# Moving the gathers for q ahead of the previous sums in a sparse graph-attention kernel

## The chip, the cores and the metric

The kernel runs on one core of one Trainium2 chip. The metric is the device time of one execution in microseconds (us). Before the change it is 1331.45 us, the median of three runs (1329.03 to 1333.0). The profiled execution spans 1331.5 us.

A core has five engines with an instruction order each: TensorE (PE, matmuls, with its weight loads shown as PEld), VectorE (DVE), ScalarE (ACT), GpSimd (POOL, which here issues the gathers) and SyncE (SP). Transfers run on 16 DMA engines.

## The reference

One attention layer over a sparse graph with 3327 nodes and 1024 features, with a normalised input and a residual. Cut to what matters:

```python
# x: (3327, 1024) f32; adj: (3327, 3327) int32, 0/1, symmetric, with the diagonal, about 17 ones a row
h = jnp.maximum(_layernorm(x, axis=-1), 0.0)
f = h @ Wf + bf
g = h @ Wg + bg
e = jax.nn.relu(f @ g.T)
scores = jnp.where(adj > 0, e, NEG)            # NEG = -9e15
attention = jax.nn.softmax(scores, axis=1)
x = x + attention @ (h @ W + bW)
```

Only the scores at the edges matter. So the kernel makes q = h A + v with A = Wf Wg^T (and the bias terms) once per node, takes the dot product of q with the rows h of the neighbours only, and sums these rows with the softmax's weights before it multiplies by W.

## The kernel before

The first part (0 to about 260 us) makes, for every node, the normalised row (`hd` in DRAM), the list of its neighbours (`pd`), and the matrix A. It sorts the nodes by degree into 26 tiles of 128 nodes; `perm[:, s]` holds the nodes of tile s. CAPS holds the largest number of neighbours of each tile, and ORDER the order in which the tiles are worked on:

```python
CAPS = [37, 25, 23, 22, 21, 21, 20, 20, 19, 19, 18, 18, 17, 17, 17, 16, 16, 15, 15, 15, 14, 14, 13, 13, 12, 11]
ORDER = [24, *range(24), 25]
ONE_CHUNK = 16
AHEAD = 3
```

The second part, which the change touches, works on one tile after the other. A tile with more than 16 neighbours is worked on in two halves; a half, or a whole small tile, is a "unit". The loop:

```python
    prepare(ORDER[0])
    prepare(ORDER[1])
    dots_of_first(ORDER[0], CAPS[ORDER[0]])
    ...
    for i, (s, k0, k1) in enumerate(units):
        last = k1 == CAPS[s]
        at = ORDER.index(s)
        dots(s, range(k0, k1))                  # gathers of neighbours' rows, dot products with q (DVE)
        softmax(s, k0, k1, last)                # exponential on ACT, the rest on DVE
        if i + 1 < len(units):
            s2, a, b = units[i + 1]
            dots(s2, range(a, min(b, a + AHEAD)))   # the first three of the next unit
        if last and at:
            finish(ORDER[at - 1])               # scatter the results of the tile before
        combine(s, k0, k1, last)                # weighted sum of the rows
        if last:
            project(s)                          # times W; adds x
            if at + 2 < NT:
                prepare(ORDER[at + 2])          # q of the tile two ahead
            ...
```

`prepare` gathers the neighbours' list `pi` and the tile's own rows `hp`, transposes these on PE and multiplies them by A:

```python
    psp = ctx.enter_context(tc.tile_pool(name="ps", bufs=2))       # pi
    gpool = ctx.enter_context(tc.tile_pool(name="G", bufs=26))     # all gathered rows, hp too
    qpool = ctx.enter_context(tc.tile_pool(name="q", bufs=2))
    hTpool = ctx.enter_context(tc.tile_pool(name="hT", bufs=1))

    def gather(to, table, idx, **kw):
        return nc.gpsimd.indirect_dma_start(out=to, ..., in_=table, ...)   # profile line L686

    def transposed2(to, of):
        for g in range(0, KD, 4):
            ps = p_t.tile([P, 4, P], FP, name="ps_t")
            for k in range(4):
                nc.tensor.transpose(ps[:, k, :], of[:, (g + k) * P : (g + k + 1) * P], ident)   # L698
            nc.scalar.copy(to[:, g : g + 4, :], ps)                                             # L699

    def prepare(s):
        e = st[s] = {}
        pi = psp.tile([P, PW], I32, name="pi")
        gather(pi, pd[:, :], perm[:, s : s + 1])
        hp = gpool.tile([P, D], FP, name="G")
        gather(hp, hd[:, :], perm[:, s : s + 1])
        hT = hTpool.tile([P, KD, P], FP, name="hT")
        transposed2(hT, hp)
        q = e["q"] = qpool.tile([P, QW], FP, name="q")
        for i, o in enumerate(range(0, QW, QB)):
            ...                                  # 8 matmuls hT x A_sb into ps_q (L731), copied to q by ACT (L735)
        ...                                      # the mask, from pi (L740)
        e["edges"] = [pi[:, k : k + 1] for k in range(KL)]
        ...                                      # longer lists, for tiles 0 and 1 only
```

The work on a neighbour k, the softmax, and the sums:

```python
    def dot(s, k):
        g = G[s, k] = gpool.tile([P, D], FP, name="G")
        st["gathered"] = gather(g, hd[:, :], e["edges"][k])
        nc.vector.tensor_tensor_reduce(junk, g, e["q"][:, :D], ...)                # L767

    def softmax(s, k0, k1, last):
        ...                                                                        # max on DVE: nm, L796
        nc.scalar.activation(sc, sc, AF.Exp, bias=nm, accum_out=l)                 # L800
        ...
        nc.vector.reciprocal(rs, l)                                                # L807
        ...

    def combine(s, k0, k1, last):
        ...
            if k in pe:                          # some neighbours: scaled on ACT, summed on PE
                nc.scalar.activation(g, g, AF.Copy, scale=p)                       # L842
                sum_transposed(e, g, e["first"], False)                            # 8 matmuls yT_ps, L826
            elif k == 0:
                nc.scalar.activation(y, y, AF.Copy, scale=p)                       # L846
            else:                                # the others: summed on DVE
                nc.vector.scalar_tensor_tensor(y, g, p, y, ...)                    # L848

    def project(s):
        sum_transposed(e, e["y"], e["first"], True)                                # yT_ps, L826
        ...                                                                        # yT, copied by ACT, L855
        for o in range(OH):
            ...                                  # 8 matmuls yT x W_sb into ps_o (L861), copied to res by ACT (L870)
        ...
            gather(r, x[:, :], perm[:, s : s + 1], compute_op=ALU.add)             # res += x
```

`finish(s)` scatters `res` to `out` (L881) and is told to be issued after the last neighbour's gather that stands before it in the source.

Of the kernel before, what the change touches and what calls it, by code (L numbers as in the profile page):

```python
# [8 lines left out]
FP = mybir.dt.float32  # L9
I32 = mybir.dt.int32  # L10
# [18 lines left out]
ORDER = [24, *range(24), 25]  # L29
# [264 lines left out]
def edge_path(ctx: ExitStack, tc: tile.TileContext, x, adj, Wf, bf, Wg, bg, W, bW, out, flag):  # L294
# [12 lines left out]
    N, D = x.shape  # L307
    O = W.shape[1]
    P = 128
# [4 lines left out]
    NT = (N + P - 1) // P  # L314
    OH = O // CB
    SW = -(-N // SEG)
    PW = KL + 1
# [13 lines left out]
    hd = dram.tile([N, D], FP, name="hd")  # L331
    pd = dram.tile([N, PW], I32, name="pd")
# [11 lines left out]
    perm = const.tile([P, NT], I32, name="perm")  # L344
# [6 lines left out]
    with ExitStack() as part1:  # L351
# [288 lines left out]
        ps = p_mm.tile([P, CB], FP, name="ps_A")  # L640
# [27 lines left out]
    nc.sync.dma_start(W_sb, W.rearrange("(k p) o -> p k o", p=P))  # L668
    bWb = ctx.enter_context(tc.tile_pool(name="bW", bufs=1)).tile([P, O], FP, name="bWb")
    nc.sync.dma_start(bWb, bW[None, :].to_broadcast([P, O]))  # L670
    psp = ctx.enter_context(tc.tile_pool(name="ps", bufs=2))
    gpool = ctx.enter_context(tc.tile_pool(name="G", bufs=26))
    mpool = ctx.enter_context(tc.tile_pool(name="more", bufs=1))
    qpool = ctx.enter_context(tc.tile_pool(name="q", bufs=2))
# [10 lines left out]
    def gather(to, table, idx, **kw):  # L685
        return nc.gpsimd.indirect_dma_start(  # L686
            out=to,
            out_offset=None,
            in_=table,
            in_offset=bass.IndirectOffsetOnAxis(ap=idx, axis=0),  # L690
            **kw,
# [9 lines that stand above are left out]
    st = {}  # L701
# [4 lines left out]
    def filled(pool, name, row, w, at):  # L706
        ps = pool.tile([P, CB], FP, name=name)
        if at < 2:
            nc.tensor.matmul(ps, ident, A_sb[:, 0, :CB], start=True, stop=True)
        o = at * w % row.shape[1]  # L710
        nc.scalar.copy(ps[:, :w], row[:, o : o + w])
        banks[name, at] = ps

    for at in range(2):
        filled(p_q, "ps_q", vb, QB, at)
        filled(p_o, "ps_o", bWb, CB, at)

    def prepare(s):
        e = st[s] = {}
        pi = psp.tile([P, PW], I32, name="pi")  # L720
        gather(pi, pd[:, :], perm[:, s : s + 1])
        hp = gpool.tile([P, D], FP, name="G")
        gather(hp, hd[:, :], perm[:, s : s + 1])
        hT = hTpool.tile([P, KD, P], FP, name="hT")
        transposed2(hT, hp)
        q = e["q"] = qpool.tile([P, QW], FP, name="q")
        for i, o in enumerate(range(0, QW, QB)):
            at = 3 * ORDER.index(s) + i
            ps = banks.pop(("ps_q", at))
            for k in range(KD):  # L730
                nc.tensor.matmul(  # L731
                    ps[:, :QB], hT[:, k, :], A_sb[:, k, o : o + QB], start=False, stop=(k == KD - 1),
                    skip_group_check=True,
                )
            nc.scalar.copy(q[:, o : o + QB], ps[:, :QB])  # L735
            if at + 2 < 3 * NT:
                filled(p_q, "ps_q", vb, QB, at + 2)
        df = pi.bitcast(FP)[:, KL : KL + 1]
        mask = e["mask"] = small.tile([P, KM], FP, name="mask")
        nc.vector.tensor_scalar(mask, iotak, df, NEG, op0=ALU.is_ge, op1=ALU.mult)  # L740
        e["sc"] = small.tile([P, KM], FP, name="sc")
        if s == NT - 1:
            e["x"] = gpool.tile([P, O], FP, name="G")
            gather(e["x"], x[:, :], perm[:, s : s + 1])
        e["edges"] = [pi[:, k : k + 1] for k in range(KL)]
        if s >= MORE:
            return

        ct = xpool.tile([P, O], FP, name="res")[:, : SEG * 8]
        gather(ct, cd[:, :], perm[:, s : s + 1])  # L750
        found = mpool.tile([P, KM - KL + 8], FP, name="found")
        for i in range(0, KM - KL + 8, 8):
            nc.vector.max(found[:, i : i + 8], ct)
            if i < KM - KL:
                nc.vector.match_replace(ct, found[:, i : i + 8], ct, 0.0)
        more = mpool.tile([P, KM - KL], I32, name="more")
        nc.vector.tensor_scalar(more, found[:, 8:], 1.0, -1.0, op0=ALU.max, op1=ALU.add)
        e["edges"] += [more[:, k : k + 1] for k in range(KM - KL)]

    G = {}  # L760

    def dot(s, k):
        e = st[s]
        g = G[s, k] = gpool.tile([P, D], FP, name="G")
        st["gathered"] = gather(g, hd[:, :], e["edges"][k])
        junk = jpool.tile([P, D], BF, name="junk")
        nc.vector.tensor_tensor_reduce(  # L767
            junk, g, e["q"][:, :D], 1.0, e["q"][:, D : D + 1], op0=ALU.mult, op1=ALU.add,
            accum_out=e["sc"][:, k : k + 1],
        )  # L770

    def dots_of_first(s, cap):

        e = st[s]
        for k in range(cap):
            G[s, k] = gpool.tile([P, D], FP, name="G")
            st["gathered"] = gather(G[s, k], hd[:, :], e["edges"][k])
        sums = mpool.tile([P, 3, cap], FP, name="sums")
        for i, o in enumerate(range(0, D, QB)):
            w = min(QB, D - o)  # L780
            for k in range(cap):
                junk = jpool.tile([P, D], BF, name="junk")
                nc.vector.tensor_tensor_reduce(
                    junk[:, :w], G[s, k][:, o : o + w], e["q"][:, o : o + w], 1.0,
                    e["q"][:, D : D + 1] if o + w == D else 0.0, op0=ALU.mult, op1=ALU.add,
                    accum_out=sums[:, i, k : k + 1],
                )
        nc.vector.tensor_reduce(e["sc"][:, :cap], sums.rearrange("p c k -> p k c"), AX.X, ALU.add)

    def softmax(s, k0, k1, last):  # L790

        e = st[s]
        sc = e["sc"][:, k0:k1]
        nc.vector.scalar_tensor_tensor(sc, sc, 0.0, e["mask"][:, k0:k1], op0=ALU.max, op1=ALU.add)
        nm = small.tile([P, 1], FP, name="nm")
        nc.vector.tensor_reduce(nm, sc, AX.X, ALU.max, negate=True)  # L796
        if k0:
            nc.vector.tensor_tensor(nm, nm, e["nm"], op=ALU.min)
        l = small.tile([P, 1], FP, name="l")
        nc.scalar.activation(sc, sc, AF.Exp, bias=nm, accum_out=l)  # L800
        if k0:
            al = small.tile([P, 1], FP, name="al")
            nc.scalar.activation(al, e["nm"], AF.Exp, bias=nm, scale=-1.0)
            nc.vector.scalar_tensor_tensor(l, e["l"], al, l, op0=ALU.mult, op1=ALU.add)
        if last:
            rs = small.tile([P, 1], FP, name="rs")
            nc.vector.reciprocal(rs, l)  # L807
            if k0:
                nc.vector.tensor_tensor(al, al, rs, op=ALU.mult)
            nc.vector.tensor_scalar(sc, sc, rs, None, op0=ALU.mult)  # L810
        if k0:
            nc.scalar.activation(e["y"], e["y"], AF.Copy, scale=al)
        e["nm"], e["l"] = nm, l
# [64 lines left out]
    def finish(s):  # L878

        with tc.issue_after(st["gathered"].ins):  # L880
            ins = nc.gpsimd.indirect_dma_start(  # L881
                out=out[:, :],
                out_offset=bass.IndirectOffsetOnAxis(ap=perm[:, s : s + 1] if s < N // P else final, axis=0),
                in_=st[s]["r"],
                in_offset=None,
                bounds_check=None if s < N // P else N - 1,
                oob_is_err=s < N // P,
            )
        tc.declare_no_dep(ins.ins, group="results", reason="other rows")
        tc.add_to_no_dep_group("results", ins.ins)  # L890
# [19 lines left out]
    def dots(s, ks):  # L910
        for k in ks:
            if (s, k) not in done:
                done.add((s, k))
                dot(s, k)

    prepare(ORDER[0])
    prepare(ORDER[1])
    dots_of_first(ORDER[0], CAPS[ORDER[0]])
    done.update((ORDER[0], k) for k in range(CAPS[ORDER[0]]))
    for i, (s, k0, k1) in enumerate(units):  # L920
        last = k1 == CAPS[s]
        at = ORDER.index(s)
        dots(s, range(k0, k1))
        softmax(s, k0, k1, last)
        if i + 1 < len(units):
            s2, a, b = units[i + 1]
            dots(s2, range(a, min(b, a + AHEAD)))
        if last and at:
            finish(ORDER[at - 1])
        combine(s, k0, k1, last)  # L930
        if last:
            project(s)
            if at + 2 < NT:
                prepare(ORDER[at + 2])
            if at + 2 == NT - 1:
                bad = failed()
# [41 lines left out]
```

## Time and profile before

| engine | busy us | share of the span | instructions |
|---|---|---|---|
| PE | 1105.4 | 83% | 4312 |
| PEld | 690.2 | 52% | 4312 |
| DVE | 1184.0 | 89% | 2377 |
| ACT | 580.1 | 44% | 923 |
| POOL | 847.2 | 64% | 677 |

"Busy" is the time in which an engine has an instruction at work. The profile names an instruction by its line in the kernel (L698), its engine, its operation, and the tiles it writes and reads: `ps_t<-ident,G` is a transpose of a gathered row tile. `G<-hd,pi` is a gather of neighbours' rows by a list `pi`, `G<-hd,perm` the gather of a tile's own rows for q, `pi<-pd,perm` the gather of the lists. What stands in square brackets behind an instruction in the timeline is how long its engine stood idle ahead of it, and what it waited for. A row of the waits gives the instruction, what it waited for, the sum in us, the number of waits and the longest one.

### The profile page before, as it was taken

The numbers are of one execution on the slowest core, as the hardware profiler recorded it, in microseconds if no ns is written. First come the engines' busy times: TensorE is split into PE (matmuls) and PEld (weight loads), VectorE is DVE, ScalarE is ACT, GpSimd is POOL, SyncE is SP. The second block draws the span as 40 slices with busy tenths as digits, with TensorE's granted clock in tenths as the row PEclk, the third lists the DMA queues.
The fourth block names the chain that finished last, engine by engine and source line by source line (L and its number), as shares of the span: only waits on it lengthen the run. The fifth ranks groups of instructions, "written<-read, shape, count | busy, mean of one in ns | idle before, by whom it ended". The sixth has DMA issues, their size and how long they took to land. (4 is left out here: it accounts for less than half of the span.)

```text
span 1331.5 us, 14117 instructions
## 1 busy us (share of the span) xinstructions
PE 1105.4 (83%) x4312; PEld 690.2 (52%) x4312; DVE 1184.0 (89%) x2377; ACT 580.1 (44%) x923; POOL 847.2 (64%) x677
## 2 busy tenths in 40 slices
PE   2588897289249899898999999999999997889965
PEld 2355564056136655566555656656556554545532
DVE  4779888749988999999999999999999998889990
ACT  6778787224125533555334444444433332224210
POOL 6699888356657766666666766666665655666511
PEclk9589898589669999999999999999999998899978
DMA  9999996398659988998899888988788776868811
GB/s 356 338 374 342 393 374 218 134 376 309 207 177 333 337 284 297 330 316 308 297 313 321 319 291 309 311 296 297 263 290 284 259 253 222 269 198 274 303 32 50
DMA packets 101660, 374.45 MB, mean 281 GB/s; under 512 B 14731, under 2 KB 18474, under 8 KB 98247
## 3 DMA queue, kind: packets, MB, share of 16 engines
q0 software_dynamic: 79584, 286.77, 63.4%
q1 hardware_dynamic: 11004, 71.01, 14.0%
q10 hardware_dynamic: 10986, 15.67, 3.3%
q8 instruction: 36, 0.59, 0.2%
q14 instruction: 50, 0.41, 0.1%
HBM read 344.11 MB, written 29.30 MB: 280 GB/s over the span
## 5 line engine op out<-in xcount | busy, mean ns | idle before, releaser
L686 POOL DMA_INDIRECT G<-hd,pi x454 | 487.4, 1074 | 199.2 <-issue 102.6
L767 DVE CUSTOM_DVE_ANT_0 junk<-G,q 128x1024 bf16<-128x1024 f32 x456 | 586.5, 1286 | 8.8 <-DMA G<-hd,pi 4.3
L731 PE MATMUL ps_q<-A_sb,hT 128*128 128x342 f32 x1248 | 382.1, 460 | 11.8 <-ACT hT L699 11.7
L848 DVE SCALAR_TENSOR_TENSOR G<-G,sc 128x1024 f32<-128x1024 f32 x296 | 381.4, 1289 | 10.6 <-ACT G L846 6.8
L861 PE MATMUL ps_o<-W_sb,yT 128*128 128x512 f32 x832 | 364.4, 596 | 7.9 <-ACT yT L855 7.9
L731 PEld LDWEIGHTS ps_q<-A_sb,hT 128*128 128x128 f32 x1248 | 236.2, 193 | 136.5 <-ACT hT L699 17.8
L861 PEld LDWEIGHTS ps_o<-W_sb,yT 128*128 128x128 f32 x832 | 158.0, 191 | 202.0 <-issue 187.5
L424 POOL TENSOR_TENSOR r<-r,iotaj 128x1664 f32<-128x1664 f32 (+3 forms) x52 | 191.6, 3724 | 31.9 <-ACT r L417 31.8
L826 PE MATMUL yT_ps<-ident,G 128*128 128x128 f32 x1376 | 172.5, 281 | 28.6 <-DVE G L848 15.3
L826 PEld LDWEIGHTS yT_ps<-ident,G 128*128 128x128 f32 x1376 | 155.8, 144 | 55.3 <-ACT G L842 26.4
L842 ACT ACTIVATE G<-G,sc 128x1024 f32<-128x1024 f32 x146 | 154.9, 1136 | 0.0
L475 DVE MAX8 cand<-r 128x8 f32<-128x208 f32 (+2 forms) x416 | 121.7, 360 | 29.0 <-POOL r L424 29.0
L551 PE MATMUL ps_A<-WgT,WfT 128*128 128x342 f32 x432 | 140.5, 485 | 0.2 <-ACT WfT L532 0.2
L870 ACT COPY res<-ps_o 128x512 f32<-128x512 f32 x50 | 29.2, 585 | 255.0 <-PE ps_o L861 252.8
L551 PEld LDWEIGHTS ps_A<-WgT,WfT 128*128 128x128 f32 x432 | 86.3, 205 | 60.5 <-issue 21.1
L735 ACT COPY q<-ps_q 128x342 f32<-128x342 f32 x78 | 34.3, 440 | 172.7 <-PE ps_q L731 158.7
L698 PE MATMUL ps_t<-ident,G 128*128 128x128 f32 x208 | 31.9, 303 | 80.1 <-DMA G<-hd,perm 67.5
L881 POOL DMA_INDIRECT out_dram<-res,perm x25 | 35.6, 1424 | 84.0 <-DMA res<-in_x_dram,perm 83.7
L417 ACT ACTIVATE r<-r 128x3327 f32<-128x3327 int32 (+4 forms) x28 | 77.8, 2781 | 1.5 <-ACT xt L461 0.5
L686 POOL DMA_INDIRECT res<-in_x_dram,perm x25 | 43.1, 1724 | 54.8 <-ACT res L870 49.9
L698 PEld LDWEIGHTS ps_t<-ident,G 128*128 128x128 f32 x208 | 27.3, 157 | 88.8 <-issue 74.5
L699 ACT COPY hT<-ps_t 128x512 f32<-128x512 f32 x52 | 29.2, 588 | 100.4 <-PE ps_t L698 100.4
(132 smaller groups left out, 669.4 us busy)
## 6 DMA issues: line engine op xcount, KB each, us to landing
r<-in_adj_dram SPq DMA_DIRECT2D x25, 1663.5 KB, 10.9
xt<-in_x_dram SPq DMA_DIRECT2D x25, 512.0 KB, 9.2
hd<-xt ACTq DMA_DIRECT2D x25, 512.0 KB, 7.7
G<-hd,pi POOLq DMA_INDIRECT x454, 6.2
wr<-in_L_gnn_Wg_dram SPq DMA_DIRECT2D x8, 512.0 KB, 5.8
wr<-in_L_gnn_Wf_dram SPq DMA_DIRECT2D x8, 512.0 KB, 8.1
W_sb<-in_L_gnn_W_dram SPq DMA_DIRECT2D x1, 4096.0 KB, 17.9
cd<-cand ACTq DMA_DIRECT2D x25, 64.0 KB, 7.6
```

What stands on the lines that cost most here:

```text
L417: nc.scalar.activation(r[:n, b:e], a[:n, b:e], AF.Sign, accum_out=to)
L424: nc.gpsimd.tensor_mul(r[:n, b:e], r[:n, b:e], iotaj[:n, : e - b])
L475: nc.vector.max(cand[:n, s * 8 : s * 8 + 8], r[:n, s * SW : min(N, (s + 1) * SW)])
L551: nc.tensor.matmul(ps[:, :QB], WfTs[c][:, k, :], WgT[:, k, o : o + QB], start=(k == 0), stop=(k == KD - 1))
L686: return nc.gpsimd.indirect_dma_start(out=to, out_offset=None, in_=table, in_offset=bass.IndirectOffsetOnAxis(ap=idx, axis=0), **kw,)
L698: nc.tensor.transpose(ps[:, k, :], of[:, (g + k) * P : (g + k + 1) * P], ident)
L731: nc.tensor.matmul(ps[:, :QB], hT[:, k, :], A_sb[:, k, o : o + QB], start=False, stop=(k == KD - 1), skip_group_check=True,)
L767: nc.vector.tensor_tensor_reduce(junk, g, e["q"][:, :D], 1.0, e["q"][:, D : D + 1], op0=ALU.mult, op1=ALU.add, accum_out=e["sc"][:, k : k ...
L826: nc.tensor.matmul(e["yT"][:, c, :], g[:, c * P : (c + 1) * P], ident, is_transpose=True, start=(first and c % 4 == 0), stop=(last and c % ...
L842: nc.scalar.activation(g, g, AF.Copy, scale=p)
L848: nc.vector.scalar_tensor_tensor(y, g, p, y, op0=ALU.mult, op1=ALU.add)
L861: nc.tensor.matmul(ps, yT[:, k, :], W_sb[:, k, o * CB : (o + 1) * CB], start=False, stop=(k == KD - 1), skip_group_check=True,)
```

## The change

The two gathers at the head of `prepare` become a function of their own, `fetch`. It is called behind the softmax of the last unit of a tile, for the tile two ahead: in front of the first three gathers of the next unit, the scatter of results, the sums and the product with W. `prepare` stays where it was and finds list and rows fetched. As the list of the tile two ahead may now be fetched while the list of the present tile and that of the next are held, the lists get three buffers in place of two. The purpose is to have the rows at hand when TensorE comes to transpose them.

```diff
--- before.py
+++ after.py
@@ -668,7 +668,7 @@
     nc.sync.dma_start(W_sb, W.rearrange("(k p) o -> p k o", p=P))
     bWb = ctx.enter_context(tc.tile_pool(name="bW", bufs=1)).tile([P, O], FP, name="bWb")
     nc.sync.dma_start(bWb, bW[None, :].to_broadcast([P, O]))
-    psp = ctx.enter_context(tc.tile_pool(name="ps", bufs=2))
+    psp = ctx.enter_context(tc.tile_pool(name="ps", bufs=3))
     gpool = ctx.enter_context(tc.tile_pool(name="G", bufs=26))
     mpool = ctx.enter_context(tc.tile_pool(name="more", bufs=1))
     qpool = ctx.enter_context(tc.tile_pool(name="q", bufs=2))
@@ -715,14 +715,19 @@
         filled(p_q, "ps_q", vb, QB, at)
         filled(p_o, "ps_o", bWb, CB, at)
 
+    def fetch(s):
+
+        e = st[s] = {}
+        pi = e["pi"] = psp.tile([P, PW], I32, name="pi")
+        gather(pi, pd[:, :], perm[:, s : s + 1])
+        hp = e["hp"] = gpool.tile([P, D], FP, name="G")
+        gather(hp, hd[:, :], perm[:, s : s + 1])
+
     def prepare(s):
-        e = st[s] = {}
-        pi = psp.tile([P, PW], I32, name="pi")
-        gather(pi, pd[:, :], perm[:, s : s + 1])
-        hp = gpool.tile([P, D], FP, name="G")
-        gather(hp, hd[:, :], perm[:, s : s + 1])
+        e = st[s]
+        pi = e["pi"]
         hT = hTpool.tile([P, KD, P], FP, name="hT")
-        transposed2(hT, hp)
+        transposed2(hT, e["hp"])
         q = e["q"] = qpool.tile([P, QW], FP, name="q")
         for i, o in enumerate(range(0, QW, QB)):
             at = 3 * ORDER.index(s) + i
@@ -913,7 +918,9 @@
                 done.add((s, k))
                 dot(s, k)
 
+    fetch(ORDER[0])
     prepare(ORDER[0])
+    fetch(ORDER[1])
     prepare(ORDER[1])
     dots_of_first(ORDER[0], CAPS[ORDER[0]])
     done.update((ORDER[0], k) for k in range(CAPS[ORDER[0]]))
@@ -922,6 +929,8 @@
         at = ORDER.index(s)
         dots(s, range(k0, k1))
         softmax(s, k0, k1, last)
+        if last and at + 2 < NT:
+            fetch(ORDER[at + 2])
         if i + 1 < len(units):
             s2, a, b = units[i + 1]
             dots(s2, range(a, min(b, a + AHEAD)))
```

## The prediction

> **What bounds the kernel now.** I read the page first, then a table of stretches, then the waits and the timelines of the stretch where an engine stands still. The page gives VectorE (DVE) 89% of the span and TensorE (PE) 83%, and neither average says where a change can act. The table of stretches does. Its columns are the stretch, its length, and the busy time of PE, weight loads, DVE, ScalarE (ACT), GpSimd (POOL), each with a count, then the granted clock, the DMA share and GB/s.
>
> ```profile
> 480.00:900.00 420.00, 397.37 (x1660) 250.64 (x1659) 418.33 (x654) 191.33 (x304) 281.85 (x260) 0.99 0.90 309
> 900.00:1100.00 200.00, 192.88 (x753) 119.09 (x752) 190.52 (x274) 76.07 (x129) 122.07 (x108) 1.00 0.82 273
> 1100.00:1200.00 100.00, 80.66 (x281) 49.34 (x280) 81.05 (x120) 26.36 (x49) 57.92 (x50) 0.90 0.72 232
> ```
>
> From 480 to 900 us DVE is idle for 420.00 - 418.33 = 1.7 us. Nothing that only moves a gather can win there. From 900 to 1100 PE is at 96% and DVE at 95%: both are nearly full. From 1100 to 1200 both drop to 81%, although POOL and the DMA engines have room. That is the place to look. The waits of DVE in the stretch from 1085 to 1230 us name what stops it:
>
> ```profile
> DVE rs L807 <- ACT sc L800: 17.8, 3, 6.2
> DVE G L848 <- ACT G L846: 0.7, 1, 0.7
> ```
>
> Three waits, 17.8 us, all at the reciprocal after the softmax's exponential. ACT is not busy there (26.36 of 100 us), so something holds it up in its own order. The timelines of PE and of POOL show the first case:
>
> ```profile
> 1111.78 1.51 PE L698 MATMUL ps_t<-ident,G 128*128 128x128 f32 x6 [8.59 <-DMA G<-hd,perm]
> 1113.08 1.91 PE L826 MATMUL yT_ps<-ident,G 128*128 128x128 f32 x8
> ...
> 1116.27 13.90 PE L861 MATMUL ps_o<-W_sb,yT 128*128 128x512 f32 x32
> ```
>
> ```profile
> 1123.33 0.59 ACT L870 COPY res<-ps_o 128x512 f32<-128x512 f32 x1 [6.74 <-PE ps_o L861]
> 1123.95 0.59 ACT L711 COPY ps_o<-bWb 128x512 f32<-128x512 f32 x1
> 1124.48 0.30 ACT L800 ACTIVATE sc<-sc,nm 128x15 f32<-128x15 f32 x1
> ```
>
> The row `ps_t` is the transpose of the rows that make q. It waited 8.59 us for its gather. Behind it in PE's order stand the last sum of tile 18 (`yT_ps`) and tile 18's product with W (`ps_o`). Behind that product in ACT's order stands the exponential of tile 19, and DVE waits for that one 6.25 us. So one late gather of q's rows blocks three engines in turn. The same happens at 1152.16 us (PE waits 6.14, DVE 5.55) and at 1190.48 (4.55 and 6.04). DVE: 6.25 + 5.55 + 6.04 = 17.84 us. PE: 8.59 + 6.14 + 4.55 = 19.28 us.
>
> Why is the gather late? POOL's timeline before the second case:
>
> ```profile
> 1134.93 0.97 POOL L686 DMA_INDIRECT G<-hd,pi  x1 [0.30 <-issue]
> 1139.21 1.42 POOL L881 DMA_INDIRECT out_dram<-res,perm  x1 [3.31 <-DMA res<-in_x_dram,perm]
> 1141.26 1.75 POOL L686 DMA_INDIRECT G<-hd,pi  x1 [0.63 <-issue]
> 1143.32 0.94 POOL L686 DMA_INDIRECT G<-hd,pi  x1 [0.30 <-issue]
> 1144.56 0.94 POOL L686 DMA_INDIRECT G<-hd,pi  x1 [0.30 <-issue]
> 1145.80 0.95 POOL L686 DMA_INDIRECT pi<-pd,perm  x1 [0.31 <-issue]
> 1147.06 0.94 POOL L686 DMA_INDIRECT G<-hd,perm  x1 [0.30 <-issue]
> ```
>
> I take 1134.93 for the last gather of tile 20. Then come the scatter of results, which waits for its rows, the first three gathers of tile 21, the list `pi` of tile 22, and only then the rows for q of tile 22. PE, whose order has these transposes next, starts them at 1152.16, 5.1 us after the gather was issued.
>
> **What the Trainium skill says.** "Perfetto Trace Analysis", section on the SWDGE DMA instruction: the profiled end of such an instruction is the end of descriptor generation, and not of the data movement. The trace agrees: 0.94 us for the instruction, a median of 6.2 us to landing for `G<-hd,pi`. "DMA: Bandwidth & Descriptors", rules for kernel authors: to overlap a DMA with compute, issue it early and wait late. That is what the change tries, and the 8.59 us of PE is what the present place costs. "Perfetto Trace Analysis", optimization strategy: a gap that repeats on the engine that should be saturated can mean that there is no room for the next tile's buffer. In part this holds: `pi` waited 24.0 us in 11 cases for the landing of gathers that read the buffer it takes, which the third buffer cures. The rows for q need no list, though, and their delay in the lines above is one of place.
>
> **The change, part by part.** No instruction is added or removed: 26 list gathers, 26 row gathers and all matmuls stay. What moves is the place of two gathers per tile (24 of the 26 tiles; the first two keep theirs) and a wait for a buffer.
>
> 1. *How much sooner.* For tile 22 the three gathers of tile 21 no longer stand in front: issued at 1141.26, 1143.32 and 1144.56, with `pi` at 1145.80, they take 4.5 us. If the scatter also stays behind, `pi` can go right after 1134.93 + 0.97 = 1135.90, and the rows at 1135.90 + 0.30 + 0.95 + 0.30 = 1137.5, which is 9.6 us sooner. So 4.5 to 9.6 us. For tile 21, where four gathers stand between 1099.16 and the list at 1105.21, three of them out of the way make 1105.21 - 1100.43 = 4.8 us. For tile 23 the list went out at 1175.83 and the rows at 1182.71, behind two gathers and the gather of x; right behind the list is 1177.2, or 5.5 us sooner.
> 2. *What that is worth.* For tile 21 the wait of 8.59 us would still be 3.8; the sums of tile 18 were ready at 1105.2 (end of the last DVE sum), so they start some 4.6 us sooner than 1113.08, and DVE's 6.25 us shrink by 4.6. For tile 22 PE's 6.14 us shrink by 4.5 to 6.14, DVE's 5.55 by 4.5 to 5.55: I take 5.2. For tile 23 PE's 4.55 us go, DVE gets 4.5 of its 6.04. Sum: 4.6 + 5.2 + 4.5 = 14.3 us. DVE is full around these waits (28.93 of 29 us between two of them), so I count them on the path at full value.
> 3. *The start.* The rows for tile 2 went out at 378.93, behind gathers issued at 368.86, 373.19 and 375.59, and PE stood 42.59 us for them. But DVE was busy 38.24 of the 40 us from 340 to 380, so these 42.59 us are not on the path. Only a later wait of DVE for ACT, 2.73 us at 394.74, hangs on the transposes: I count 1 us of it.
> 4. *What it costs.* The next tile's first three gathers go out two instructions later, 2 x 1.25 = 2.5 us. In the tail they have room: issued at 1141.26, first used by DVE at 1153.42, 12.2 us for a landing of 6.2. At the start they have little: DVE waited there 4.3 us in four waits for gathers (401 to 415 us), and 1 us may be added. The rows hold one of the 26 buffers of G some 5 to 10 us longer per tile of 35 us, 0.2 of a buffer on average: I count 0.5 us.
> 5. *Order.* The order on the engines is fixed when the program is built and isn't that of the source: transposes for tile 21 stand before tile 18's product. With the gather earlier, the whole order is made anew, and some waits will come back at another place. I take off 1.5 us for that.
>
> Sum: 14.3 + 1 - 1 - 0.5 - 1.5 = 12.3 us, some 13 with the shortened waits for lists. From 1331.45 us that makes 1318 us.
>
> **Rivals.** *(a) PE becomes the bound.* From 900 to 1100 us PE is at 96%, and a tile there costs it 14.07 (ps_q) + 13.90 (ps_o) + 1.04 (ps_t) + some 4 (sums) = 33 us, as much as DVE's 15 x 1.33 + 11 x 1.2 = 33. If PE ran on without a gap, DVE would wait for it instead. Against it: PE loses the same 19.28 us of idle, and after 1200 its tiles follow at 28 to 29 us. If this came true in full, half of the gain would go: 1325. *(b) The gather isn't in front where it matters.* Rows need a buffer of G, and POOL waits for those (67.9 us for DVE's sums to release them; 11.21 us at 1129.24). If the buffer and not the place is the limit, the rows come no sooner: 1330. Against it: in the lines above the three gathers in front got their buffers at once (waits of 0.30 and 0.63). *(c) The new order is worse.* A transpose that is believed ready too soon can be put even further ahead of sums and products, and stall PE for the buffer of hT or for the rows again. Each such stall cost 5 to 6 us of DVE; three or four more in a tail of ten tiles make 1345 to 1350. *(d) More than the three waits.* If the early hold-ups (2.73 + 4.3 us at the start) go as well, and all of 17.84, it is 1307.
>
> **Range and chances.** I give (a) 0.25, (b) 0.15, (c) 0.12 with mild and bad forms, the main line and (d) the rest. Main line with its neighbours spans 1312 to 1325; (d) sets the lower end at 1306, a mild (c) the upper at 1331. Two per cent are 26.6 us, more than all of 17.84 + 2.73 + 4.3 = 24.9 us of waits that I can point at, so faster by over 2% needs a gain that I don't see: 0.10. Slower by over 2% (1358) needs the bad form of (c): 0.04. Within: 0.86.
>
> **What would show each step right or wrong.** Step 1: rows for q of tiles 20 to 23 issued ahead of the next tile's first gathers, and the wait of `ps_t` for `G<-hd,perm` after 900 us down from 19.3 to under 6. Step 2: DVE's wait of `rs` for `sc`, 17.8 us in three cases, down to under 5, and DVE at 93% or more from 1100 to 1200. Step 3: the 42.6 us of PE at the start shorter by about 10, with DVE's busy share there as it was. Step 4: DVE's wait for gathers near 4 to 6 us in all. The lists' wait for landings, 24.0 us, near 0. The prediction is wrong if `rs` still waits 10 us or more, if PE's wait moves to another operand with DVE waiting as long, or if DVE's idle time between 480 and 900 grows beyond 5 us.

## The result, and the profile after

The changed kernel takes 1312.75 us (median of five runs, 1309.46 to 1315.63), 18.7 us less than before: 0.986 of the time before, with a 95% interval of 0.984 to 0.988. The prediction was 1318 us, a gain of 13.4. The profiled execution spans 1309.4 us; it lies 22.1 us under that of the kernel before, more than the medians do, as the one execution was slower than its kernel's median and the other faster. Behind `fetch` the line numbers are five higher: L826 is now L831, L861 is L866, and L807 is L812.

The table of stretches (stretch, length, busy time of PE, weight loads, DVE, ACT and POOL with counts, granted clock, DMA share, GB/s):

```profile
480.00:900.00 420.00, 397.33 (x1658) 250.75 (x1657) 418.20 (x655) 192.69 (x306) 298.68 (x262) 0.99 0.91 313
900.00:1100.00 200.00, 190.06 (x747) 117.81 (x745) 190.55 (x274) 75.75 (x129) 120.34 (x108) 1.00 0.80 267
1100.00:1200.00 100.00, 96.61 (x348) 58.26 (x349) 98.53 (x143) 32.51 (x57) 63.77 (x56) 0.98 0.82 280
```

The first two stretches are as before. In the third DVE goes from 81.05 to 98.53 us and PE from 80.66 to 96.61. DVE's waits from 1063 to 1208 us, the counterpart of the stretch shown before:

```profile
DVE rs L812 <- ACT sc L805: 1.2, 2, 0.9
DVE G L853 <- ACT G L851: 1.2, 1, 1.2
```

The 17.8 us of three waits are down to 1.2, the longest to 0.9. The timeline of PE at the transposes of tiles 21, 22 and 23 (the bracket gives the stand ahead and its cause):

```profile
1102.07 0.95 PE L698 MATMUL ps_t<-ident,G 128*128 128x128 f32 x6 [3.78 <-DMA G<-hd,perm]
1102.82 1.91 PE L831 MATMUL yT_ps<-ident,G 128*128 128x128 f32 x8
...
1106.09 13.90 PE L866 MATMUL ps_o<-W_sb,yT 128*128 128x512 f32 x32
...
1135.69 1.04 PE L698 MATMUL ps_t<-ident,G 128*128 128x128 f32 x8
...
1167.64 1.04 PE L698 MATMUL ps_t<-ident,G 128*128 128x128 f32 x8
```

The first stand of 8.59 us is 3.78 now, the second (6.14 us) and the third are gone. And POOL's timeline around the rows of tile 22:

```profile
1124.76 0.97 POOL L686 DMA_INDIRECT G<-hd,pi  x1 [0.30 <-issue]
1128.37 0.97 POOL L886 DMA_INDIRECT out_dram<-res,perm  x1 [2.65 <-DMA res<-in_x_dram,perm]
1129.65 0.96 POOL L686 DMA_INDIRECT G<-hd,perm  x1 [0.30 <-issue]
1130.92 2.00 POOL L686 DMA_INDIRECT G<-hd,pi  x1 [0.30 <-issue]
1133.22 0.94 POOL L686 DMA_INDIRECT G<-hd,pi  x1 [0.30 <-issue]
1134.47 0.94 POOL L686 DMA_INDIRECT G<-hd,pi  x1 [0.30 <-issue]
```

The rows now stand right behind the scatter, 1.28 us after its start, and the three gathers of tile 21 follow. Before, they came 1147.06 - 1139.21 = 7.85 us after it. The list, which has a third buffer, went out well ahead, at 1112.04.

Where the time went can be read off without any model, because the order of DVE's instructions is the same in both kernels, instruction for instruction. So each softmax can be set against itself. The table gives the start of the DVE instruction that opens it (L794, now L799), in us after the first one (308.38 before, 306.60 now; the 1.8 us ahead of that lie in the first part, which the change doesn't touch):

| softmax of | before | changed | difference |
|---|---|---|---|
| tile 24 | 0 | 0 | 0 |
| tile 1, first half | 102.89 | 100.57 | -2.3 |
| tile 19 | 807.43 | 804.37 | -3.1 |
| tile 20 | 844.83 | 836.51 | -8.3 |
| tile 21 | 882.04 | 867.43 | -14.6 |
| tile 22 | 916.76 | 896.17 | -20.6 |
| tile 25, the last | 971.21 | 950.60 | -20.6 |

Of 20.6 us, 17.5 are won in three steps of 5.3 to 6.3 us behind the softmax of tiles 19, 20 and 21, 2.3 at the start, and 0.8 little by little between.

### The profile page after: what moved, and what is told of

Its sections match the earlier page's. It is cut to its first block, busy times and chain, and to the rows that moved or that the text cites. A ratio compares the mean times of both kernels' runs of the same rounds, so it can differ in the third digit from the quotient of the medians.

```text
span 1309.4 us, 14125 instructions
## 1 busy us (share of the span) xinstructions
PE 1105.0 (84%) x4312; PEld 691.6 (53%) x4312; DVE 1182.3 (90%) x2377; ACT 580.3 (44%) x923; POOL 857.4 (65%) x677
## 4 chain that ended last, share of the span: by engine, by line
DVE 33%; issue 25%; DMA 14%; PE 13%; POOL 8%; ACT 6%; POOLq 0%; ACTq 0%; DVEq 0%; SPq 0%
DVE G L853 16%; DMA G<-hd,pi 7%; DVE junk L772 6%; POOL G L686 5%; DVE cand L475 4%; PE yT_ps L831 4%; PE ps_o L866 3%; PE ps_q L736 3%; PE ps_A L551 2%; POOL r L424 2%; ACT G L847 2%; DVE sc L772 1%; DMA res<-in_x_dram,perm 1%; ACT r L417 1%; DMA r<-in_adj_dram 1%
## 5 line engine op out<-in xcount | busy, mean ns | idle before, releaser
L686 POOL DMA_INDIRECT G<-hd,pi x454 | 498.2, 1097 | 201.5 <-issue 99.8
L736 PE MATMUL ps_q<-A_sb,hT 128*128 128x342 f32 x1248 | 374.7, 454 | 13.8 <-ACT hT L699 13.8
L866 PE MATMUL ps_o<-W_sb,yT 128*128 128x512 f32 x832 | 367.3, 600 | 9.2 <-ACT yT L860 9.2
L736 PEld LDWEIGHTS ps_q<-A_sb,hT 128*128 128x128 f32 x1248 | 233.0, 190 | 136.0 <-ACT hT L699 19.7
L866 PEld LDWEIGHTS ps_o<-W_sb,yT 128*128 128x128 f32 x832 | 158.8, 192 | 205.1 <-issue 189.0
L831 PE MATMUL yT_ps<-ident,G 128*128 128x128 f32 x1376 | 176.7, 286 | 37.4 <-ACT G L847 20.7
L831 PEld LDWEIGHTS yT_ps<-ident,G 128*128 128x128 f32 x1376 | 161.2, 148 | 62.9 <-ACT G L847 35.3
```

What stands on the lines that cost most here:

```text
L686: return nc.gpsimd.indirect_dma_start(out=to, out_offset=None, in_=table, in_offset=bass.IndirectOffsetOnAxis(ap=idx, axis=0), **kw,)
L736: nc.tensor.matmul(ps[:, :QB], hT[:, k, :], A_sb[:, k, o : o + QB], start=False, stop=(k == KD - 1), skip_group_check=True,)
L831: nc.tensor.matmul(e["yT"][:, c, :], g[:, c * P : (c + 1) * P], ident, is_transpose=True, start=(first and c % 4 == 0), stop=(last and c % ...
L866: nc.tensor.matmul(ps, yT[:, k, :], W_sb[:, k, o * CB : (o + 1) * CB], start=False, stop=(k == KD - 1), skip_group_check=True,)
```

## The experiments

Two theories stood against each other at first. **Place of the rows**: the rows for q come in time because they are gathered ahead of the next tile's first three gathers; the rest of the change is not needed. **Room for the lists**: the third list buffer takes away the 24.0 us that POOL waited for lists, and that is the gain. The edit of e1 is to the kernel before, all others are to the changed kernel. Ratios are to the kernel before on the same chip, with 95% intervals; they leave out executions in a slower state of the chip, so they can differ from the ratio of the medians. On the chips of e5 to e8, e11 and e12 even the kernel before took 1373 to 1376 us, and the traces of these runs have long stands of ScalarE for which they name no cause. Their times are a result about these chips, taken up at the end; they cannot tell the theories apart.

### e1: three list buffers alone

```diff
-    psp = ctx.enter_context(tc.tile_pool(name="ps", bufs=2))
+    psp = ctx.enter_context(tc.tile_pool(name="ps", bufs=3))
```

> The kernel before with three list buffers in place of two and nothing moved. Theory 'place of the rows' (the gain comes from the rows for q being gathered ahead of the next tile's first three neighbour gathers): the rows keep their place behind those three, so 1331 us within 4, and DVE still waits 15 to 18 us for the exponential after 1100 us. Theory 'room for the lists' (the lists' 24 us of waits for a free buffer hold GpSimd up): most of the gain is here, 1313 to 1318 us. Some small gain from lists alone: 1326 to 1330.

Measured: 1332.79 us, ratio 1.001 (1.000 to 1.002). The waits for lists of the whole execution, first in the kernel before, then here:

```profile
POOL pi L686 <- DMA G<-hd,pi: 24.0, 11, 2.9
```

```profile
POOL pi L686 <- DMA G<-hd,pi: 6.3, 3, 3.6
```

And those of DVE from 900 us on:

```profile
DVE rs L807 <- ACT sc L800: 17.6, 6, 7.0
```

POOL's wait for lists falls from 24.0 to 6.3 us, and the time doesn't move. DVE waits as before.

### e2: only the rows early

```diff
     def fetch(s):
         e = st[s] = {}
-        pi = e["pi"] = psp.tile([P, PW], I32, name="pi")
-        gather(pi, pd[:, :], perm[:, s : s + 1])
         hp = e["hp"] = gpool.tile([P, D], FP, name="G")
         gather(hp, hd[:, :], perm[:, s : s + 1])
     def prepare(s):
         e = st[s]
-        pi = e["pi"]
+        pi = psp.tile([P, PW], I32, name="pi")
+        gather(pi, pd[:, :], perm[:, s : s + 1])
```

The lists have two buffers here.

> Only the gather of the rows moves to the new place; the list's gather stays in prepare, with two list buffers. 'Place of the rows': all of the gain, 1312 to 1316 us, DVE's wait for the exponential under 3 us. 'Room for the lists': no gain, 1328 to 1333 us.

Measured: 1314.34 us, ratio 0.986 (0.984 to 0.988), the ratio of the whole change. DVE's wait for the exponential from 900 us on is 2.5 us.

### e3: only the list early

```diff
     def fetch(s):
         e = st[s] = {}
         pi = e["pi"] = psp.tile([P, PW], I32, name="pi")
         gather(pi, pd[:, :], perm[:, s : s + 1])
-        hp = e["hp"] = gpool.tile([P, D], FP, name="G")
-        gather(hp, hd[:, :], perm[:, s : s + 1])
     def prepare(s):
         e = st[s]
         pi = e["pi"]
+        hp = e["hp"] = gpool.tile([P, D], FP, name="G")
+        gather(hp, hd[:, :], perm[:, s : s + 1])
```

> Only the gather of the list moves, with three list buffers; the gather of the rows stays in prepare. 'Place of the rows': 1328 to 1333 us, DVE's three waits for the exponential as before, 15 to 18 us. 'Room for the lists': 1313 to 1318 us.

Measured: 1332.95 us, ratio 1.001 (1.000 to 1.002), with 14.8 us of waits for the exponential from 900 us on, in the trace of the fastest execution: nothing is won.

### e4: both early, two list buffers

```diff
-    psp = ctx.enter_context(tc.tile_pool(name="ps", bufs=3))
+    psp = ctx.enter_context(tc.tile_pool(name="ps", bufs=2))
```

> The changed kernel with two list buffers in place of three: both gathers in the new place. 'Place of the rows': the third buffer is not needed, 1311 to 1315 us, equal to the changed kernel's 1312.75 within its spread; GpSimd may wait again some 10 to 25 us for lists, off the path. 'Room for the lists': 1325 to 1332 us.

Measured: 1314.77 us, ratio 0.986 (0.983 to 0.989). The wait for lists, over the whole execution:

```profile
POOL pi L686 <- DMA G<-hd,pi: 44.0, 13, 4.4
```

POOL waits longer for lists than in any other of these kernels, 44.0 us, more than I had expected, and the kernel is as fast as the changed one within the intervals. With e1 and e3 this settles that "room for the lists" is wrong: taking that wait away wins nothing, and nearly doubling it costs nothing that shows.

### e5 and e9: the new place for the last five tiles alone

```diff
-        if last and at + 2 < NT:
+        if last and at + 2 < NT and at + 2 >= 21:
             fetch(ORDER[at + 2])
 ...
             if at + 2 < NT:
+                if not (at + 2 >= 21):
+                    fetch(ORDER[at + 2])
                 prepare(ORDER[at + 2])
```

> The changed kernel, but list and rows go to the new place only for the last five tiles worked on (21, 22, 23 and 25, and 20); for all tiles before, both gathers stay at the head of prepare. If the gain is the three removed waits of the tail: 1314 to 1318 us, with TensorE still standing over 40 us for the rows near 342 us. If the gain is spread over all tiles or comes from the start: 1322 to 1330 us.

Measured: 1394.88 us, ratio 1.010 (1.003 to 1.018): slower than the kernel before on this chip, which neither expectation had. The same kernel on another chip:

> The tail-only kernel once more, as on the chip of the last runs even the kernel before took 1373 us. List and rows go to the new place only for the last five tiles worked on. If the gain is the three removed waits of the tail: 1314 to 1318 us, DVE's wait for the exponential after 1100 us under 4 us, TensorE still standing over 40 us for the rows near 342 us. If the gain is spread over all tiles or comes from the start: 1322 to 1330 us.

Measured: 1316.26 us, ratio 0.989 (0.987 to 0.991). DVE's waits from 900 us on, and PE's wait for the rows over the whole execution:

```profile
DVE rs L812 <- ACT sc L805: 1.3, 4, 0.3
```

```profile
PE ps_t L698 <- DMA G<-hd,perm: 51.6, 4, 43.7
```

From the softmax of tile 19 to that of tile 22 it takes 90.66 us, against 109.33 before and 91.80 in the changed kernel: the whole gain of the tail. PE still stands 43.7 us for the rows of tile 2 at the start. The ratio is 0.003 above that of the whole change, some 4 us, and the intervals overlap a little at 0.987 to 0.988; so of the 18.7 us some 14 to 15 are the tail's, and up to 4 may lie at the start and in the middle.

### e6: the complement

The condition of e5 turned round: the new place up to tile 19, the old one for the last five.

> The complement: the new place for all tiles up to tile 19, the old one for the last five. If the gain is that of the tail: 1327 to 1331 us, DVE's wait for the exponential after 1100 us 15 to 18 us as before. If it comes from the start: 1313 to 1320 us.

Measured: 1405.38 us, ratio 1.020 (1.014 to 1.026): again slower than the kernel before on this chip. The tail can be read by itself. PE's transposes of tiles 21, 22 and 23 (the first instructions of each), and DVE's reciprocals of tiles 19, 20 and 21:

```profile
1182.97 1.51 PE L698 MATMUL ps_t<-ident,G 128*128 128x128 f32 x6 [6.22 <-DMA G<-hd,perm]
1221.60 1.97 PE L698 MATMUL ps_t<-ident,G 128*128 128x128 f32 x8 [4.65 <-DMA G<-hd,perm]
1261.10 1.97 PE L698 MATMUL ps_t<-ident,G 128*128 128x128 f32 x8 [5.12 <-DMA G<-hd,perm]
```

```profile
1195.84 0.16 DVE L812 RECIPROCAL rs<-l 128x1 f32<-128x1 f32 x1 [5.56 <-ACT sc L805]
1231.74 0.16 DVE L812 RECIPROCAL rs<-l 128x1 f32<-128x1 f32 x1 [4.76 <-ACT sc L805]
1271.94 0.16 DVE L812 RECIPROCAL rs<-l 128x1 f32<-128x1 f32 x1 [7.91 <-ACT yT L860]
```

With the old place for these tiles the three stands and the three waits are back (the third wait is put down to ACT's copy of yT, which stands right ahead of the exponential). From the softmax of tile 19 to that of tile 22 it takes 110.1 us, where e5 on the same chip takes 94.4: one trace each, but the tail's waits come and go with the place of its own gathers here too.

### e7, e8 and e10: behind one, behind two of the three gathers

```diff
-        if last and at + 2 < NT:
-            fetch(ORDER[at + 2])
         if i + 1 < len(units):
             s2, a, b = units[i + 1]
+            dots(s2, range(a, min(b, a + 2)))      # e7: a + 1
+            if last and at + 2 < NT:
+                fetch(ORDER[at + 2])
             dots(s2, range(a, min(b, a + AHEAD)))
```

> Both gathers stand behind the first of the next unit's three gathers, in front of the other two. The rows go out some 1.3 us later per tile than in the changed kernel. If place alone counts and some slack is left: 1313 to 1317 us, DVE's wait for the exponential in the tail 1 to 4 us. If the full distance is needed: 1318 to 1325 us.

Measured: 1400.54 us, ratio 1.017 (1.008 to 1.027), slower than the kernel before on this chip. Its stretch from the softmax of tile 19 to that of tile 22 took 95.3 us, little more than the 94.4 of e5.

> As the run before, but behind two of the three gathers: some 2.6 us later per tile than in the changed kernel. If the waits grow with the number of gathers in front: 1317 to 1325 us, DVE's wait for the exponential in the tail 5 to 11 us, between the 0.9 us of the changed kernel and the 17.8 us of the kernel before. If the wait is all or nothing: 1313 or 1331 us.

Measured: 1399.34 us, ratio 1.010 (1.005 to 1.016), slower than the kernel before on this chip. The same kernel, behind two, on another chip:

> Both gathers behind two of the next unit's three gathers, once more. If the waits grow with the number of gathers in front: 1316 to 1325 us, DVE's wait for the exponential in the tail 4 to 11 us, between the 0.9 us of the changed kernel and the 17.8 us of the kernel before. If it is all or nothing: 1313 or 1331 us.

Measured: 1320.12 us, ratio 0.992 (0.990 to 0.994), between before and changed, as the waits are. PE's timeline at the transposes of tiles 21 and 22, and DVE's at the reciprocal of tile 19:

```profile
1108.75 1.51 PE L698 MATMUL ps_t<-ident,G 128*128 128x128 f32 x6 [7.27 <-DMA G<-hd,perm]
...
1144.84 1.09 PE L698 MATMUL ps_t<-ident,G 128*128 128x128 f32 x8 [1.75 <-DMA G<-hd,perm]
```

```profile
1121.97 0.17 DVE L812 RECIPROCAL rs<-l 128x1 f32<-128x1 f32 x1 [4.98 <-ACT sc L805]
```

Put the three kernels in a row, at tile 21's rows: PE stands 3.78, 7.27 and 8.59 us (changed, behind two, before), and DVE then waits 0.9, 4.98 and 6.25. Both rise together, with some 2.3 to 2.9 us of PE's stand free of charge (the slack). In e9 a stand of 2.04 us there cost DVE nothing, which fits. At tile 22 1.75 us of PE cost nothing. So the waits aren't all or nothing: at tile 21's rows, about each microsecond of lateness beyond the slack is one of DVE. The slack isn't a constant. In e1 and e4 it is 1.6 and 1.8 us at the same place (stands of 8.57 and 3.62 us, waits of 7.01 and 1.80), and in the kernel before it is 0.6 us at tile 22 and none at tile 23, where DVE waited longer (6.04) than PE stood (4.55).

The stretch from the softmax of tile 19 to that of tile 22 sorts these kernels by the place of the rows: 109.3 us before, 108.5 in e1 and 105.4 in e3 with the old place; 96.7 behind two; 91.8 changed, 91.8 in e2, 92.8 in e4 and 90.7 in e9 with the new one.

### e11: one step sooner still

```diff
+        if last and at + 2 < NT:
+            fetch(ORDER[at + 2])
         dots(s, range(k0, k1))
         softmax(s, k0, k1, last)
-        if last and at + 2 < NT:
-            fetch(ORDER[at + 2])
```

> List and rows one step sooner still: in front of the remaining gathers of the tile's own last unit. If the waits that the rows' place causes are used up in the changed kernel (0.9 us left), nothing more is to be had: 1310 to 1316 us, or slower, up to 1325, as the buffer of G is held longer and the order of the engines is made anew. If lateness of the rows still costs at the start (TensorE stands 32 us there): 1305 to 1309 us.

Measured: 1402.27 us, ratio 1.018 (1.012 to 1.024), slower than the kernel before on this chip; here the order of DVE's instructions changes too. Whether an earlier place would win more on a chip of the other kind stays open.

### e12: fewer VectorE sums ahead of the last products

```diff
-        m = min(max(0, CAPS[s] - 12), k1 - k0 - 2) if s != ORDER[0] else (k1 - k0) // 2
+        m = min(max(5 if s == 23 else 0, CAPS[s] - 12), k1 - k0 - 2) if s != ORDER[0] else (k1 - k0) // 2
```

The same sums are made, four more of them on TensorE.

> The changed kernel, with five of tile 23's thirteen weighted rows summed on TensorE in place of one: four VectorE sums (1.28 us each) fewer ahead of the last two products with W, four transposed sums (1.04 us each) more on TensorE, which stands 9.2 us there. If VectorE's sums of tile 23 set the end: 4.5 to 5.1 us faster than the changed kernel, 1307 to 1309 us. If TensorE's two last products set it: no change, 1312 to 1314 us.

Measured: 1392.21 us, ratio 1.002 (0.998 to 1.006). As a time it decides nothing. Its last stretch can be read by itself: in DVE's timeline from the softmax of tile 23 to the last sum with x, first in the changed kernel, then here.

```profile
1233.74 0.16 DVE L799 SCALAR_TENSOR_TENSOR sc<-sc,mask 128x13 f32<-128x13 f32 x1
...
1296.76 0.69 DVE L871 TENSOR_TENSOR res<-ps_o,G 128x512 f32<-128x512 f32 x1 [6.18 <-PE ps_o L866]
```

```profile
1325.23 0.22 DVE L799 SCALAR_TENSOR_TENSOR sc<-sc,mask 128x13 f32<-128x13 f32 x1
...
1379.91 0.69 DVE L871 TENSOR_TENSOR res<-ps_o,G 128x512 f32<-128x512 f32 x1 [6.17 <-PE ps_o L866]
```

63.02 us there, 54.68 here. In e5, on a chip of the same kind, the stretch took 62.46 us, so it doesn't seem to be the chip. DVE's sums of tile 23 do seem to set the end, by one trace, and more strongly than I had worked out: 8 us where I expected 5, and the difference is not explained. A whole kernel faster than the changed one has not been shown, as the total didn't move on that chip.

## Why the prediction was right, step by step

**What bounds the kernel.** Right. The stretch from 1100 to 1200 us was where the gain lay, and the rows for q were what came late: with the rows in time all three waits fell together, and with the rows a little late (e10) the first came back in proportion. But "the same happens" was not exact. Only the first wait ran over the product with W. At the second and the third the late rows held up PE's products for q, ACT's copy of q behind them, and the exponential behind that copy, as ACT's timeline of the kernel before shows:

```profile
1160.41 0.45 ACT L735 COPY q<-ps_q 128x342 f32<-128x342 f32 x1 [5.66 <-PE ps_q L731]
...
1161.27 0.30 ACT L800 ACTIVATE sc<-sc,nm 128x14 f32<-128x14 f32 x1
```

PE's next product with W began only at 1163.96.

**Step 1, how much sooner.** Right for tile 22: 6.6 us sooner against the scatter (7.85 - 1.28), inside 4.5 to 9.6. For tile 21 the rows went out 2.75 us after the scatter's start in place of 9.57, so 6.8 us sooner, where I had 4.8. First before, then changed:

```profile
1096.90 1.96 POOL L881 DMA_INDIRECT out_dram<-res,perm  x1 [4.00 <-DMA res<-in_x_dram,perm]
...
1106.47 0.94 POOL L686 DMA_INDIRECT G<-hd,perm  x1 [0.30 <-DMA G<-hd,pi]
```

```profile
1092.82 1.18 POOL L886 DMA_INDIRECT out_dram<-res,perm  x1 [4.78 <-DMA res<-in_x_dram,perm]
...
1095.57 2.00 POOL L686 DMA_INDIRECT G<-hd,perm  x1 [0.30 <-issue]
```

I took away three gathers, but the list's place in front was freed as well (1.26 us), and the next gather followed the scatter 0.8 us sooner.

**Step 2, what it is worth.** The mechanism was right, the size too small: 14.3 us predicted, 17.5 measured. I had left 1.65, 0.35 and 1.5 us of the three waits; 0.9 was left in all, and a wait of 0.7 us that followed the second one went too. The term most mis-sized is that of tile 23. There I held DVE's gain to PE's stand, 4.5 of 6.04 us, and all 6.04 went. PE began these transposes at 1190.48 before, together with the softmax of tile 21 at 1190.42, and at 1167.64 in the changed kernel, 6.4 us ahead of it at 1174.03. PE's gains at the tiles before seem to add up here; no run separates them.

That PE's stand left at tile 21 is 3.78 us, as good as my 3.8, is luck. The rows went out 2 us sooner than I had counted, but PE came to them 0.8 us sooner too, and could begin 6.50 us after their issue in place of 5.31.

**Step 3, the start.** PE's stand for the rows of tile 2 fell from 42.59 to 32.1 us, as predicted, and won little by itself. DVE's 2.73 us at the transposes went altogether, and a wait of 1.76 us just ahead of it grew to 2.60. Up to the first softmax of tile 1 that made 2.3 us in place of the 1 us I had counted.

**Steps 4 and 5, the costs.** Both were too pessimistic. DVE's wait for gathers at the start stayed at 4.1 us (4.3 before). The feared new order didn't come: DVE's order is the same throughout, ACT's and PE's differ up to tile 2, and later only in how PE's products for q are cut around the transposes of the last tiles; what moved is POOL's order. I took off 3 us in these steps for nothing measurable. The wait for lists, which I expected near 0, fell from 24.0 to 6.7 us.

By the traces, then, step 2 gave 3.2 us more than predicted and the start 1.3, and the 3 us of deductions were not lost. That is more than the 5.3 us between prediction and result, as the two traced executions lie further apart than the medians; how these 5.3 us divide is not shown to the microsecond.

**The rivals.** (a) PE as the next bound: not up to 1200 us, where DVE reaches 98.5% with PE at 96.6%. (b) The buffers of G: POOL does wait longer for DVE's sums to free them (83.0 us, 67.9 before), but the rows got theirs in time. (c) A worse order: no. (d) More than the main line: nearly so; the kernel came to lie between the main line's 1318 and the 1307 of (d). The third buffer, which I had credited with the lists' part (under 1 us), is worth nothing that e1, e2 and e4 can show.

## What to carry to other kernels

When an engine that is nearly full waits for one that isn't, follow the second engine's own order back to the first instruction in it that waited for data; the cure may be the place of one transfer in the issuing engine's order. A wait's length alone doesn't give its worth: 24 to 44 us of waiting for list buffers cost nothing, while late rows for which PE stood 19.3 us in three places cost DVE 17.5 us. If one engine's instruction order is the same in two kernels, set its landmarks against each other; the differences show where the time was won.

## What had not been expected

The result depends on more than the kernel. On chips where the kernel before takes 1373 to 1376 us, all five kernels that move the gathers and nothing else (e5, e6, e7, e8, e11) came out 1.0 to 2.0% slower than it, with intervals above 1, and e12 the same as it. The tail-only kernel was at 1.010 there and at 0.989 on another chip, the kernel behind two at 1.010 and 0.992. ScalarE there stood for up to 17 us at a time ahead of copies (in e5 16.58 at 301.89): 26 stands of over 2 us after 260 us with no engine or transfer named, 177 us in all, and none in the traces of the kernel before, the changed kernel and e9. What stands behind them is not known. The changed kernel itself was not run on such a chip, so its gain of 18.7 us is shown only for chips on which the kernel before takes some 1331 us.
